# Clipping the ratio of layer 2 on ScalarE: a Relu with shifted logarithms in place of a VectorE maximum

## The chip, the cores and the metric

The kernel runs on one core of a Trainium2 chip. The core has five engines that work side by side, each through its own instruction queue and strictly in the order of that queue: TensorE (PE in the profile, its weight loads PEld), VectorE (DVE), ScalarE (ACT), GpSimd (POOL) and SyncE (SP, which issues most DMAs). They wait for each other through semaphores. The metric is the device time of one execution in microseconds (us), taken as the median of several runs; lower is better.

## What is computed

Four graph layers run one after another on 32 graphs of 512 nodes with 64 features; each layer is followed by x = layernorm(x + layer(x)). Layer 0 is a normalised neighbour mean, layer 1 a Chebyshev filter of order 4, layer 2 hyperbolic attention and layer 3 a weighted quantile of the neighbours with a small network behind it. The change lies in layer 2, which needs for every pair of nodes (i, j) the distance of the two points in the Poincaré ball:

```python
def _artanh(x):
    return jnp.arctanh(jnp.clip(x, -1.0 + 1e-07, 1.0 - 1e-07))

def logmap(p1, p2, c):
    sub = mobius_add(-p1, p2, c)
    sub_norm = _norm(sub)
    sqrt_c = c ** 0.5
    return 2.0 / sqrt_c / lambda_x(p1, c) * _artanh(sqrt_c * sub_norm) * sub / sub_norm
```

artanh(r) is half of ln(1 + r) - ln(1 - r). The clip keeps r below 1, so that the second logarithm stays finite. All 512 x 512 pairs of a graph need it, but the matrix is symmetric: the kernel computes the upper triangle in blocks (512 + 384 + 256 + 128 = 1280 columns on 128 partitions) and gets the rest by transposing.

## The kernel before

For each of the 32 graphs the kernel records the operations of seven lanes, in Python functions: `front` (loads, layers 0 and 1), `pairs` (layer 2's pair matrix), `tail` (the rest of layer 2), `graph`, `gather` and `sort` (layer 3's ranks, one-hot gather and sorting network), and for each pair of graphs `head` (the sorting network's narrow part, the network and the output). Helpers record them: `tt` (line 448, a VectorE operation on two tensors), `ts` (452, on one tensor and constants), `stt` (455), `act` (483, ScalarE), `mm` (502, matmul), `tr` (507, transpose), `gp` (POOL). Nearly every instruction of the profile therefore has a helper's line, and the tile's name tells what it is.

The order is not that of the recording. The class `Order` plans it at build time. It gives every operation a duration by formula (`ts` on f32: 0.07 + 0.52e-3 us per element; `act`: 0.12 + 0.83e-3 us per element, plus 0.09 for each bias or scale that is a tile), a due time from `STAGES` and a period of 80 us per graph, and then lets each engine take, whenever it is free, the ready operation with the earliest due time. The engines' queues are then pinned to that order. One more rule bears on PE: where the plan has a gap on PE, it puts filler matmuls on a scratch bank, `stay_active` (lines 1458 and 1459), one for each 0.11 us of the gap beyond its first 0.3 us. So the number of fillers in PE's queue tells how much waiting of PE the order was laid out with.

Around the change, in `pairs`: E holds the clipped-below squared distance, X its product with a denominator. The work is done in two parts of 640 columns (`parts2`). ScalarE makes R = X^-1/2 through Ln and Exp and W = R²/2; VectorE refines that with one Newton step (W·X, then R, each 128 x 640) and multiplies E by R, which gives minus the ratio r; then comes the clip; ScalarE takes both logarithms, into W and X; VectorE subtracts them and multiplies with R into Q. Q goes through PE (transposes of blocks, of `pairs_L`) to the attention weights. The tiles `EX`, `RW` and `Q` have one buffer each, so the next graph's pairs wait until this graph's have been read.

Of the kernel before, what the change touches and what calls it, by code (L numbers as in the profile page):

```python
# [8 lines left out]
F32 = mybir.dt.float32  # L9
# [5 lines left out]
AF = mybir.ActivationFunctionType  # L15
OP = mybir.AluOpType
# [4 lines left out]
P = 128  # L21
# [382 lines left out]
def tile_adj_resnorm(ctx: ExitStack, tc: tile.TileContext, x, adj, nodemask, w1k, b1k, att_w, att_b,  # L404
                     w1, b1, w2, b2, out):
    nc = tc.nc
# [12 lines left out]
    const = ctx.enter_context(tc.tile_pool(name="const", bufs=1))  # L419
# [7 lines left out]
    def width(a):  # L427
        n = 1
        for d in a.ap[1:]:
            n *= d[1]  # L430
        return n

    def vec(f, out, ins, one=False, scalars=(), reads=None, **kw):

        n = width(reads if reads is not None else out)
        tiles = [out] + list(ins)
        rate = 1.04e-3
        if not any(a.space == PSUM for a in tiles):
            half = all(a.dtype in (F16, BF16) for a in tiles)
            if one:  # L440
                rate = 0.26e-3 if half else 0.52e-3
            elif half:
                rate = 0.52e-3
        sc = [a for a in scalars if isinstance(a, bass.AP)]
        seq.op("DVE", 0.07 + n * rate + 0.065 * len(sc), 0.085, f, [out], list(ins) + sc)

    def tt(out, a, b, op):
        vec(lambda: nc.vector.tensor_tensor(out, a, b, op=op), out, [a, b])  # L448

    def ts(out, a, s1, s2, op0, op1=None):  # L450
        kw = {} if op1 is None else {"op1": op1}
        vec(lambda: nc.vector.tensor_scalar(out, a, s1, s2, op0=op0, **kw), out, [a], True, (s1, s2))  # L452

    def stt(out, a, s, b, op0, op1):
        vec(lambda: nc.vector.scalar_tensor_tensor(out, a, s, b, op0=op0, op1=op1), out, [a, b], False, (s,))  # L455
# [21 lines left out]
    def act(out, a, f, bias=None, scale=1.0, accum_out=None, after=None):  # L477
        sc = [x for x in (bias, scale) if isinstance(x, bass.AP)]
        kw = {k: v for k, v in (("bias", bias), ("accum_out", accum_out)) if v is not None}
        n = width(out)  # L480
        table = "exp" if f in (AF.Ln, AF.Exp) else "sig" if f in (AF.Sigmoid, AF.Tanh) else None
        seq.op("ACT", 0.12 + n * 0.83e-3 + 0.09 * len(sc) + (0.2 if accum_out is not None else 0.0),
             0.3, lambda: nc.scalar.activation(out, a, f, scale=scale, **kw), [out, accum_out], [a, after] + sc, table)  # L483
# [119 lines left out]
    ts(last, kf[:, 16:].unsqueeze(2).to_broadcast([P, K - 16, 8]), 2.0, 1.0, op0=OP.mult, op1=OP.add)  # L603
    mhalf = const.tile([P, T], F32, name="mhalf")
    nc.gpsimd.memset(mhalf, -0.5)
    tiny = const.tile([P, 1], F32, name="tiny")
    nc.vector.memset(tiny, 1e-36)
    onesb = const.tile([P, P], BF16, name="onesb")
    nc.vector.memset(onesb, 1.0)
    zero = const.tile([P, 2 * P], BF16, name="zero")  # L610
# [96 lines left out]
    def wide(name, tag=None):  # L707
        return seq.tile(pools["small"], [P, T, D], F32, name, 1, tag)
# [260 lines left out]
    def pairs(b, res):  # L969
# [65 lines left out]
        E, X = EX[:, 0, :], EX[:, 1, :]  # L1035
        RW = seq.tile(mid, [P, 2, NS], F32, "RW", 1)
        R, W = RW[:, 0, :], RW[:, 1, :]
        for j in range(T):
            n = N - j * P
            o = slice(OB[j], OB[j + 1])  # L1040
# [12 lines left out]
        for o in parts2:  # L1053

            tt(W[:, o], W[:, o], X[:, o], op=OP.mult)
            stt(R[:, o], W[:, o], -1.5, R[:, o], op0=OP.add, op1=OP.mult)
            tt(E[:, o], E[:, o], R[:, o], op=OP.mult)
            ts(E[:, o], E[:, o], -1.0 + 1e-7, None, op0=OP.max)
            act(W[:, o], E[:, o], AF.Ln, bias=1.0)
            act(X[:, o], E[:, o], AF.Ln, bias=1.0, scale=-1.0)  # L1060
        Q = seq.tile(mid, [P, T, N], F32, "Q", 1)
        for o in parts2:
            tt(W[:, o], W[:, o], X[:, o], op=OP.subtract)
        for j in range(T):
            o = slice(OB[j], OB[j + 1])
# [37 lines left out]
        v = wide("v")  # L1103
# [320 lines left out]
    with ExitStack() as fast:  # L1424
# [42 lines left out]
        for b in range(B):  # L1467
            if b % 2 == 0:
                both = {"ends": []}
            res = dict(both)  # L1470
            seq.batch = b
            for lane, f in (("front", front), ("pairs", pairs), ("graph", stage_graph), ("gather", gather), ("sort", sort)):
                seq.lane = lane
                f(b, res)
            both["ends"].append((res["slots"][1], res["x3"][0]))
            both.update(ohm=res["ohm"], ap=res["ap"])
            if b == B - 1:
                both["spots"] = spots(both["ends"])
            if b % 2:
                seq.lane = "head"  # L1480
                head(b, both)
# [144 lines left out]
    with tc.If(flagv > 0):  # L1626
        with ExitStack() as slow:
# [24 lines left out]
            for h in range(4):  # L1652
                t = cst.tile([P, T, QC * ROWS], BF16, name=f"parts{h}")
# [32 lines left out]
def build(inputs):  # L1686
    import numpy as np
    import concourse.bacc as bacc

    nc = bacc.Bacc("TRN2", target_bir_lowering=False, num_devices=1)  # L1690
    arrays, args = {}, []
    for name in _INS:
        a = np.ascontiguousarray(inputs[name])
        if a.dtype == np.bool_:
            a = a.view(np.uint8)
        arrays[f"in_{name}_dram"] = a
        args.append(nc.dram_tensor(f"in_{name}_dram", a.shape, mybir.dt.from_np(a.dtype), kind="ExternalInput").ap())
    args.append(nc.dram_tensor("out_0_dram", inputs["x"].shape, F32, kind="ExternalOutput").ap())
    with tile.TileContext(nc) as tc:
        tile_adj_resnorm(tc, *args)  # L1700
    return nc, arrays
# [8 lines left out]
```

## Time and profile before

| what | us |
| --- | --- |
| median of 3 runs (2572.68 to 2582.51) | 2580.22 |
| the profiled execution's own time | 2575.55 |
| its span, first to last instruction | 2573.7 |
| PE busy, share of the span | 2413.6 (94%) |
| DVE busy | 2382.1 (93%) |
| ACT busy | 1837.6 (71%) |
| POOL busy | 848.9 (33%) |
| granted TensorE clock, mean | 0.979 |

PE's busy time includes the fillers, and the ends of matmuls are modelled. A DVE or ACT record reaches some way into the next one of its engine: a record is longer than what the instruction costs in its queue. DMA plays no part: the queues' packets take 6.5% of the 16 DMA engines.

### The profile page before, as it was taken

The numbers are of one execution on the slowest core, as the hardware profiler recorded it, in microseconds if no ns is written. First come the engines' busy times: TensorE is split into PE (matmuls) and PEld (weight loads), VectorE is DVE, ScalarE is ACT, GpSimd is POOL, SyncE is SP. The second block draws the span as 40 slices with busy tenths as digits, with TensorE's granted clock in tenths as the row PEclk, the third lists the DMA queues.
The fourth block names the chain that finished last, engine by engine and source line by source line (L and its number), as shares of the span: only waits on it lengthen the run. The fifth ranks groups of instructions, "written<-read, shape, count | busy, mean of one in ns | idle before, by whom it ended". The sixth has DMA issues, their size and how long they took to land.

```text
span 2573.7 us, 56084 instructions
## 1 busy us (share of the span) xinstructions
PE 2413.6 (94%) x19895; PEld 1635.0 (64%) x19918; DVE 2382.1 (93%) x8937; ACT 1837.6 (71%) x4156; POOL 848.9 (33%) x2007
## 2 busy tenths in 40 slices
PE   7999989999999999999999999999999999999997
PEld 6766666656666666666666666666666666666555
DVE  4669999999999999999999999999999999999996
ACT  5766677777677777777677776877777777777761
POOL 1234434333234333323343433333333333333210
PEclk9999999999899999999999999998999999999998
DMA  1100000000000000000000000000000000000000
GB/s 39 36 22 21 22 14 13 24 22 26 20 15 19 16 26 22 24 10 22 22 20 26 22 22 22 12 22 20 26 22 18 16 18 24 20 12 3 8 5 8
DMA packets 119723, 49.98 MB, mean 19 GB/s; under 512 B 53740, under 2 KB 119436, under 8 KB 119436
## 3 DMA queue, kind: packets, MB, share of 16 engines
q1 hardware_dynamic: 118272, 46.15, 6.5%
q8 instruction: 158, 2.59, 0.4%
q14 instruction: 129, 1.06, 0.1%
q10 hardware_dynamic: 1164, 0.18, 0.0%
HBM read 37.93 MB, written 8.39 MB: 18 GB/s over the span
## 4 chain that ended last, share of the span: by engine, by line
DVE 73%; PE 20%; ACT 4%; issue 2%; POOL 1%; DMA 0%; ACTq 0%; DVEq 0%
DVE SB L448 17%; DVE SH L448 10%; DVE gather_oh L452 7%; PE pairs_bank L502 4%; DVE pairs_Q L448 4%; PE front_bank L502 4%; PE graph_bank L502 3%; PE gather_bank L502 3%; DVE pairs_RW L448 3%; DVE sort_prod L448 3%; DVE pairs_Wt L455 3%; DVE pairs_L L455 2%; PE head_bank L502 2%; DVE pairs_RW L455 2%; DVE pairs_EX L448 1%
## 5 line engine op out<-in xcount | busy, mean ns | idle before, releaser
L448 DVE TENSOR_TENSOR SB<-SB 128x92 f32<-128x92 f32 (+11 forms) x1424 | 566.8, 425 | 12.6
L502 PE MATMUL gather_bank<-gather_oh,tail_x3h 128*64 128x448 f16 (+5 forms) x5376 | 522.0, 319 | 5.6 <-ACT SB L483 4.2
L502 PEld LDWEIGHTS <-tail_x3h 128*64 128x64 bf16 x5376 | 294.7, 110 | 201.8 <-issue 95.7
L448 DVE TENSOR_TENSOR SH<-SH 128x128 f32<-128x128 f32 (+10 forms) x1744 | 341.6, 247 | 7.8
L502 PE MATMUL pairs_bank<-pairs_FT 67*128 67x512 f32 (+7 forms) x768 | 323.0, 522 | 16.6 <-DVE pairs_EX L455 9.4
L452 DVE TENSOR_SCALAR gather_oh<-graph_slot 128x256 f16<-128x256 f16 (+9 forms) x864 | 257.0, 337 | 19.1 <-PE gather_bank L502 17.0
L502 PE MATMUL front_bank<-front_AT,front_y 128*64 128x256 f32 x1536 | 193.5, 387 | 16.5 <-DVE front_y L448 15.5
L502 PEld LDWEIGHTS pairs_bank<-pairs_FT 67*128 67x128 f32 (+1 forms) x768 | 132.3, 196 | 85.3 <-issue 22.7
L502 PEld LDWEIGHTS front_bank<-front_AT,front_y 128*64 128x64 f32 x1536 | 118.1, 138 | 72.7 <-DVE front_y L448 18.9
L502 PE MATMUL graph_bank<-graph_perm,graph_V 128*128 128x512 f16 x512 | 141.6, 384 | 17.4 <-DVE graph_perm L452 16.0
L502 PEld LDWEIGHTS <-graph_nbT 128*128 128x128 f16 x1536 | 113.2, 99 | 57.7 <-issue 15.3
L1458 PE MATMUL PA<-zero 128*128 128x256 bf16 x1022 | 141.5, 280 | 0.1
L502 PEld LDWEIGHTS front_bank<-XA,front_AT 128*128 128x128 f32 x1024 | 126.2, 192 | 15.7 <-issue 6.6
L471 POOL TENSOR_TENSOR tail_nr<-tail_nr,tail_y 128x4 f32<-128x4 f32 x96 | 37.1, 386 | 285.6 <-DVE tail_y L461 230.4
L719 POOL TENSOR_TENSOR front_rs<-front_var,mhalf 128x4 f32<-128x4 f32 x64 | 81.5, 1273 | 145.7 <-DVE front_var L452 130.1
L502 PE MATMUL pairs_bank<-FLS,pairs_Wt 128*128 128x66 f32 x1024 | 123.8, 275 | 2.7 <-DVE pairs_Wt L455 2.2
L502 PEld LDWEIGHTS pairs_bank<-FLS,pairs_Wt 128*128 128x128 f32 x1024 | 119.4, 192 | 9.1 <-DVE pairs_Wt L455 7.1
L502 PE MATMUL front_bank<-XA,front_AT 128*128 128x65 f32 x1024 | 124.4, 272 | 0.3 <-ACT front_AT L483 0.3
L502 PEld LDWEIGHTS <-tabs 128*128 128x128 f16 x1296 | 78.6, 98 | 62.4 <-issue 49.6
L448 DVE TENSOR_TENSOR pairs_RW<-pairs_RW,pairs_EX 128x640 f32<-128x640 f32 x128 | 103.6, 816 | 13.7 <-ACT pairs_RW L483 9.2
L1458 PEld LDWEIGHTS <-zero 128*128 128x128 bf16 x1022 | 98.9, 101 | 23.8 <-issue 8.5
L483 ACT ACTIVATE SB<-gather_bank 128x448 f32<-128x448 f32 (+2 forms) x192 | 80.9, 439 | 45.0 <-PE gather_bank L502 44.2
(355 smaller groups left out, 6451.8 us busy)
## 6 DMA issues: line engine op xcount, KB each, us to landing
front_A<-in_adj_dram SPq DMA_DIRECT2D x128, 256.0 KB, 2.7
XA<-in_x_dram SPq DMA_DIRECT2D x32, 128.0 KB, 2.3
xs<-tail_x SPq DMA_DIRECT2D x32, 128.0 KB, 1.9
out_dram<-head_zo SPq DMA_DIRECT2D x31, 128.0 KB, 2.0
out_dram<-tail_ends SPq DMA_DIRECT2D x1, 128.0 KB, 2.1
wk<-in_L_gnn_weight_dram ACTq DMA_DIRECT2D x1, 64.0 KB, 3.1
w1s<-in_L_gnn_W_dram ACTq DMA_DIRECT2D x2, 32.0 KB, 1.9
attw<-in_L_gnn_att_W_dram ACTq DMA_DIRECT2D x2, 0.2 KB, 3.5
```

Source lines behind the costliest of these rows:

```text
L448: vec(lambda: nc.vector.tensor_tensor(out, a, b, op=op), out, [a, b])
L452: vec(lambda: nc.vector.tensor_scalar(out, a, s1, s2, op0=op0, **kw), out, [a], True, (s1, s2))
L455: vec(lambda: nc.vector.scalar_tensor_tensor(out, a, s, b, op0=op0, op1=op1), out, [a, b], False, (s,))
L471: gp(lambda: nc.gpsimd.tensor_tensor(out, a, b, op=op), out, [a, b])
L483: 0.3, lambda: nc.scalar.activation(out, a, f, scale=scale, **kw), [out, accum_out], [a, after] + sc, table)
L502: return nc.tensor.matmul(out, w, a, start=start, stop=stop)
L719: seq.op("POOL", 0.8, 0.6, lambda: nc.gpsimd.tensor_tensor(y, v, mhalf, op=OP.pow), [y], [v])
L1458: return nc.tensor.matmul(PA[:, 2 * P:], zero[:, :P], zero, start=False, stop=False)
```

## The change

The maximum on VectorE goes. In its place ScalarE takes Relu(E + 1 - 2^-23), which cuts at the same place up to a shift, and the shift is taken back in the biases of the two logarithms: ln(E' + 2^-23) and ln(-E' + 2 - 2^-23). These three biases are tiles of [128, 1], set once at the start; the logarithms' bias before was the constant 1.0.

```diff
-    tiny = const.tile([P, 1], F32, name="tiny")
-    nc.vector.memset(tiny, 1e-36)
+    def constant(name, v):
+        t = const.tile([P, 1], F32, name=name)
+        nc.vector.memset(t, v)
+        return t
+
+    tiny = constant("tiny", 1e-36)
+    least, under, double = constant("least", 2.0**-23), constant("under", 1.0 - 2.0**-23), constant("double", 2.0 - 2.0**-23)
@@ pairs, for o in parts2 @@
             tt(E[:, o], E[:, o], R[:, o], op=OP.mult)
-            ts(E[:, o], E[:, o], -1.0 + 1e-7, None, op0=OP.max)
-            act(W[:, o], E[:, o], AF.Ln, bias=1.0)
-            act(X[:, o], E[:, o], AF.Ln, bias=1.0, scale=-1.0)
+            act(E[:, o], E[:, o], AF.Relu, bias=under)
+            act(W[:, o], E[:, o], AF.Ln, bias=least)
+            act(X[:, o], E[:, o], AF.Ln, bias=double, scale=-1.0)
```

Since the planner sees other durations and another engine, it lays out a new order for all engines; no constant of the planner is changed.

## The prediction

> **What bounds the kernel now.** I read the page first: busy times, then the chain of waits.
>
> ```profile
> PE 2413.6 (94%) x19895; PEld 1635.0 (64%) x19918; DVE 2382.1 (93%) x8937; ACT 1837.6 (71%) x4156; POOL 848.9 (33%) x2007
> DVE 73%; PE 20%; ACT 4%; issue 2%; POOL 1%; DMA 0%; ACTq 0%; DVEq 0%
> ```
>
> VectorE and TensorE are both nearly full, and the chain runs 73% through VectorE and 20% through TensorE. A share over the whole span mixes start, steady run and end, so the second view is busy time by stretches (span, then PE, PEld, DVE, ACT, POOL, granted clock, DMA).
>
> ```profile
> 78.00:193.00 115.00, 110.29 (x895) 80.70 (x895) 76.83 (x253) 81.28 (x189) 33.55 (x95) 1.00 0.08 23
> 193.00:2445.00 2252.00, 2129.99 (x17529) 1428.89 (x17547) 2169.64 (x8065) 1664.04 (x3787) 784.83 (x1783) 0.98 0.07 19
> ```
>
> In the steady run DVE is busy for 2169.6 of 2252 us: 82 us idle, 3.7%. PE is idle for 122 us there, and its busy time holds fillers. So VectorE is the bound, but TensorE follows within a few per cent; there is no large reserve behind it. The third view is groups, for what the change touches and for the fillers.
>
> ```profile
> L452 DVE TENSOR_SCALAR pairs_EX<-pairs_EX 128x640 f32<-128x640 f32 x64 | 30.8, 483 | 0.2
> L483 ACT ACTIVATE pairs_RW<-pairs_EX,tiny 128x640 f32<-128x640 f32 x64 | 52.9, 828 | 15.7 <-DVE pairs_EX L455 15.1
> L483 ACT ACTIVATE pairs_RW<-pairs_EX 128x640 f32<-128x640 f32 x64 | 47.0, 734 | 37.7 <-DVE pairs_EX L452 37.3
> L1458 PE MATMUL PA<-zero 128*128 128x256 bf16 x1022 | 141.5, 280 | 0.1
> ```
>
> The first is the clip that goes; the second a Ln with a tile as its bias (828 ns), the third one without (734 ns); the fourth most of the fillers, 141.5 / 1022 = 0.138 us each. The timeline tells what a record costs in its queue:
>
> ```profile
> 1185.06 0.48 DVE L452 TENSOR_SCALAR pairs_EX<-pairs_EX 128x640 f32<-128x640 f32 x1
> 1185.47 0.15 DVE L455 SCALAR_TENSOR_TENSOR front_off<-front_mv,front_rs 128x4 f32<-128x4 f32 x1
> ...
> 1187.00 0.81 ACT L483 ACTIVATE pairs_RW<-pairs_EX,tiny 128x640 f32<-128x640 f32 x1
> 1187.72 0.72 ACT L483 ACTIVATE pairs_RW<-pairs_EX 128x640 f32<-128x640 f32 x1
> 1188.34 0.72 ACT L483 ACTIVATE pairs_RW<-pairs_RW 128x640 f32<-128x640 f32 x1
> ```
>
> The next VectorE instruction starts 0.41 us after the clip, not 0.48. On ScalarE 640 columns cost 0.72 us with a tile bias and 0.62 without.
>
> **The change part by part.** (1) VectorE loses 64 clips: 64 x 0.41 = 26.2 us (30.8 by whole records, the most it can be). They stand in the full queue, with 0.2 us of idle ahead of all of them: if the queue closes up, all of it is gained. Three more memsets of [128, 1] at the start cost some 0.1 us each by the row of a like memset (112 ns), under the weights' DMA that VectorE waits 2.5 us for.
>
> (2) ScalarE gains 64 Relus with a tile bias, 64 x 0.72 = 46.1 us, and 128 logarithms grow by 0.10: 12.8 us. The compiled order shows 58 table loads instead of 57 at each of two places: 2 x 1.28 = 2.6 us. Together 61.5 us, against 736 us in which ScalarE is idle: 71% becomes 74%. This load is hidden under the other engines. The Trainium skill (ScalarE: Activation LUTs, Rules for kernel authors) speaks against it: relu and maximum belong on VectorE, which is faster per element. The rows agree, 0.41 against 0.72 us; by the rule alone the change would lose 64 x 0.31 = 20 us, by the busy times alone it would win 26.
>
> (3) The chain within a graph grows. From E·R to both logarithms there were 0.41 + 0.62 us plus the last logarithm; now there are 0.72 + 0.72, plus a last one that is 0.10 longer: 0.51 us a part, 64 parts, 33 us if every microsecond were waited for, 0 if covered. The cover is the VectorE work that stands in the queue between E·R and W - X. Adding up the compiled order with the trace's durations, it was 5.1 us on average after the clip before, and is 5.9 us now; the need is now 0.72 + 0.72 + 0.83 = 2.3 us and some handover, and 5 of the 64 parts have under 3.0. VectorE waited there 4.1 us in four waits before. I take +2 for it, of 0 to 33. Whoever stands behind these logarithms on ScalarE (evacuations of `SB`, `graph_v`, `front_AT`) is 1 us later per part, which counts where PE waits for a bank: `gather_bank` for `SB` cost PE 4.2 us in all. +0 to +4, I take +1.
>
> (4) The order. POOL (2080 instructions) and SP (268) have the same instructions in both; DVE and ACT differ by what is named above; no DMA is added, and the loads of the next graph sit on SP as before. But the queues are laid out anew, and PE's shows one thing that is no accident of naming: 1236 + 175 fillers in place of 1022 + 118, so 271 more, in 210 runs instead of 170. Its other 17,232 matmuls are the same. Between the 1,980th and the 9,240th of PE's other instructions (a stretch of the first third) fillers go from 133 to 301; ahead of transposes of `pairs_L` from 37 to 89. An order that saved VectorE's 26 us would leave PE 26 us less to wait; this one is laid out with more waiting. The price from the trace: 271 x 0.138 = 37.4 us of filler matmuls, and 40 more runs leave at least the 0.3 us each that the rule does not fill, 12 us. That is +49 us if all of it is added to PE's time and nothing else of its 160 us of idle time shrinks. It is 0 if the fillers only collect short gaps that the order had anyway; then the gain of (1) stands.
>
> I weigh it so. For: PE's time is work plus waits and ends with the span, so more waiting with the same work is a later end. Against: fillers and VectorE's idle don't go together in the trace of before. In the row 2445:2509 fillers take 14.8 us of PE, and VectorE is idle for 1.3.
>
> ```profile
> 2381.00:2445.00 64.00, 60.76 (x485) 38.05 (x482) 62.48 (x208) 49.87 (x110) 18.54 (x34) 0.97 0.03 8
> 2445.00:2509.00 64.00, 60.65 (x521) 36.87 (x520) 62.66 (x272) 39.04 (x79) 12.34 (x28) 0.95 0.02 6
> ```
>
> The net effect, (1) included, lies between -26 + 3 = -23 us (only the queue closing up) and +49 us (all the waiting real). I take +22, a little nearer to the second: the count is a fact of the new program, while the queue's closing up is a hope. It asks that VectorE's idle in the steady run goes from 82 to 82 + 26 + 22 = 130 us, 5.7% of it. Some slices of before are that idle now (386 to 450: 5.3 of 64 us; 1094 to 1158: 5.4).
>
> The sum is against the profiled execution: 2575.6 + 22 = 2597.6 (span 2595.7). That execution was 4.7 us under the median of 2580.2; on the median's scale it is 2602.
>
> **The rivals.** *VectorE closes up.* For it: 73% of the chain, 3.7% idle, 0.2 us ahead of the clip, a cover of 5.9 us. Against: 271 fillers. It gives -23 us with all of the saving, -19 by the chain's share (0.73 x 26.2): some 2557 to 2561. This is the rival on the other side; it decides if VectorE's idle in the steady run stays under 82 + 13 us.
>
> *They cancel.* Half of the waiting is real, -23 + 25 = about 0, within 0.5% (13 us), which is about what a measurement of this kernel can tell from no change. For it: two engines near full, each with another's slack.
>
> *The longer chain is the bound.* If `pairs` set the pace (single buffers of EX, RW and Q), the full 33 us of (3) would count, and no saving: 2613. Against it: the logarithms' waits of 4.1 us, and the cover; ahead of ScalarE's first Ln it was the clip that came late (37.3 us), and that was VectorE's queue, which is now shorter.
>
> *The change doesn't do what it says.* Excluded as far as the program goes: the compiled VectorE queue has no clip left.
>
> **How the numbers follow.** Slower by over 0.5%: 0.60 (the forecast 0.52, the chain as bound 0.08). Within 0.5%: 0.25. Closing up: 0.15. The range reaches from 2564, which leaves out most of the closing-up case, to 2629, the +49 us on the median's scale: some 0.8 of the chance. Slower cases alone would lie in 2594 to 2629.
>
> **What would show it.** In the profile after: no `ts` on `pairs_EX`; 64 Relus with a bias at some 0.82 us, logarithms at 0.83; DVE busy near 2382 - 26 to 31 = 2351 to 2356, ACT near 1899; fillers 1236 and 175. The forecast is right if DVE's idle grows by about 48 us or more in all, most of it between 190 and 1000 us, behind PE or `pairs`. It is wrong if DVE's idle stays near 190 us in all: then the fillers only took the place of short gaps, and the span falls by the clip's own time.

## The result and the profile after

The changed kernel takes 2605.47 us (median of 7 runs, 2596.55 to 2610.25) against 2581.86 us before on the same chip: ratio 1.0095, 95% interval 1.0075 to 1.0115, so 24 us slower. The profiled execution took 2605.47 us with a span of 2603.4 us. The page first: busy times and the chain of waits.

```profile
PE 2436.9 (94%) x20167; PEld 1663.6 (64%) x20189; DVE 2360.0 (91%) x8876; ACT 1893.2 (73%) x4222; POOL 853.6 (33%) x2007
DVE 70%; PE 20%; ACT 6%; issue 2%; POOL 1%; DMA 0%; ACTq 0%; DVEq 0%
```

VectorE does 22.1 us less work (2382.1 to 2360.0), ScalarE 55.6 us more, and the span is 29.7 us longer: VectorE's idle time went from 191.6 to 243.4 us, by 51.8. (The two profiled executions lie 29.9 us apart, 6 more than the medians.) By stretches (the columns are the stretch and its length, then busy PE, PEld, DVE, ACT and POOL, the granted clock and DMA), before:

```profile
193.00:1029.00 836.00, 788.29 (x6484) 530.23 (x6488) 804.48 (x2971) 609.38 (x1384) 296.68 (x680) 0.98 0.07 20
1029.00:2445.00 1416.00, 1341.70 (x11047) 898.66 (x11059) 1365.16 (x5095) 1054.66 (x2404) 488.14 (x1103) 0.98 0.07 18
```

and after:

```profile
193.00:1029.00 836.00, 785.27 (x6582) 537.76 (x6587) 783.06 (x2911) 618.31 (x1389) 300.94 (x668) 0.98 0.07 20
1029.00:2445.00 1416.00, 1341.67 (x11000) 901.00 (x11013) 1342.85 (x5029) 1079.95 (x2414) 485.69 (x1113) 0.98 0.07 18
```

VectorE's idle grows by 21.4 us in the first stretch (31.5 to 52.9) and by 22.3 in the second (50.8 to 73.2), 3 us ahead of 193 and 5 behind 2445. The granted clock is the same, 0.98. What VectorE waits for, in us, times and the longest, in the table of waits after:

```profile
DVE gather_oh L452 <- PE gather_bank L502: 48.5, 32, 4.3
DVE pairs_RW L448 <- ACT pairs_RW L483: 14.5, 16, 2.2
DVE pairs_EX L455 <- PE pairs_bank L502: 11.4, 10, 2.6
DVE pairs_RW L448 <- ACT pairs_EX L483: 5.1, 5, 3.0
```

and before:

```profile
DVE gather_oh L452 <- PE gather_bank L502: 17.0, 14, 2.3
DVE pairs_RW L448 <- ACT pairs_RW L483: 9.2, 8, 1.8
DVE pairs_EX L455 <- PE pairs_bank L502: 8.3, 9, 1.8
DVE pairs_RW L448 <- ACT pairs_EX L483: 4.1, 4, 1.9
```

The greatest new wait has nothing to do with the clip. It is layer 3's one-hot tile `oh`, with two buffers: VectorE can write the next one only when PE has multiplied the one before last. It grows by 31.5 us. The waits of `pairs_RW` are two. For the second logarithm (`<- ACT pairs_EX`) it goes from 4.1 to 5.1 us. The other one (`<- ACT pairs_RW`, 9.2 to 14.5) is earlier in the chain: the product W·X waits for ScalarE's W = R²/2. In the experiments, where the logarithms have lines of their own, that wait stays with the helper's line. The groups show the added and the dearer operations at the sizes forecast:

```profile
L483 ACT ACTIVATE pairs_EX<-pairs_EX,under 128x640 f32<-128x640 f32 x64 | 52.7, 827 | 41.0 <-DVE pairs_EX L448 40.7
L483 ACT ACTIVATE pairs_RW<-pairs_EX,least 128x640 f32<-128x640 f32 x64 | 52.6, 825 | 0.6
L483 ACT ACTIVATE pairs_EX<-pairs_EX,double 128x640 f32<-128x640 f32 x64 | 52.6, 824 | 0.0
```

The fillers came as forecast too, 1236 and 175, and TensorE was busy with them for 195.4 us. These are the rows after, and the row of before that the forecast did not show:

```profile
L1463 PE MATMUL PA<-zero 128*128 128x256 bf16 x1236 | 171.8, 280 | 0.4 <-issue 0.2
L1464 PE MATMUL PA<-UC,identb 128*128 128x256 f16 x175 | 23.6, 273 | 0.9 <-ACT sort_ap L483 0.9
```

```profile
L1459 PE MATMUL PA<-UC,identb 128*128 128x256 f16 x118 | 16.9, 280 | 0.5 <-ACT sort_ap L483 0.5
```

### The profile page after: what moved, and what is told of

It is laid out like the page before. It is cut to its first block, busy times and chain, and to the rows that moved or that the text cites. A ratio compares the mean times of both kernels' runs of the same rounds, so it can differ in the third digit from the quotient of the medians.

```text
span 2603.4 us, 56633 instructions
## 1 busy us (share of the span) xinstructions
PE 2436.9 (94%) x20167; PEld 1663.6 (64%) x20189; DVE 2360.0 (91%) x8876; ACT 1893.2 (73%) x4222; POOL 853.6 (33%) x2007
## 4 chain that ended last, share of the span: by engine, by line
DVE 70%; PE 20%; ACT 6%; issue 2%; POOL 1%; DMA 0%; ACTq 0%; DVEq 0%
DVE SB L448 19%; DVE SH L448 10%; DVE gather_oh L452 6%; PE front_bank L502 4%; PE gather_bank L502 4%; DVE pairs_Q L448 4%; PE pairs_bank L502 4%; PE graph_bank L502 3%; DVE pairs_Wt L455 3%; DVE pairs_RW L448 3%; DVE sort_prod L448 2%; DVE pairs_L L455 2%; PE head_bank L502 1%; ACT pairs_RW L483 1%; DVE PRS L448 1%
## 5 line engine op out<-in xcount | busy, mean ns | idle before, releaser
L502 PE MATMUL gather_bank<-gather_oh,tail_x3h 128*64 128x448 f16 (+5 forms) x5376 | 511.4, 320 | 3.6 <-ACT SB L483 2.6
L448 DVE TENSOR_TENSOR SH<-SH 128x128 f32<-128x128 f32 (+11 forms) x1744 | 343.6, 246 | 9.3 <-ACT SH L483 1.5
L502 PE MATMUL pairs_bank<-pairs_FT 67*128 67x512 f32 (+7 forms) x768 | 316.4, 516 | 19.3 <-DVE pairs_EX L455 10.1
L452 DVE TENSOR_SCALAR gather_oh<-graph_slot 128x256 f16<-128x256 f16 (+9 forms) x864 | 253.7, 338 | 50.9 <-PE gather_bank L502 48.5
L1463 PE MATMUL PA<-zero 128*128 128x256 bf16 x1236 | 171.8, 280 | 0.4 <-issue 0.2
L1463 PEld LDWEIGHTS <-zero 128*128 128x128 bf16 x1236 | 120.1, 101 | 34.8 <-issue 16.7
L448 DVE TENSOR_TENSOR pairs_RW<-pairs_RW,pairs_EX 128x640 f32<-128x640 f32 x128 | 104.3, 816 | 20.0 <-ACT pairs_RW L483 14.5
L483 ACT ACTIVATE graph_V<-graph_bank 128x512 f16<-128x512 f32 x128 | 75.7, 592 | 56.6 <-PE graph_bank L502 56.0
```

The lines of the kernel that those rows point to most:

```text
L502: return nc.tensor.matmul(out, w, a, start=start, stop=stop)
L1463: return nc.tensor.matmul(PA[:, 2 * P:], zero[:, :P], zero, start=False, stop=False)
```

## The experiments

Theory A is that of the prediction: the operations themselves win, and the order that the planner lays out for them loses more. Theory B: the longer chain Relu, Ln, Ln on ScalarE loses, whatever the order. Theory C: the 271 added fillers themselves are the cost, through the TensorE time that they take.

### The operations and the order taken apart

`Order` gets a table `queue` that lets an operation be planned for one engine and emitted on another. Everything else of the order stays: the other instructions of the five queues keep the sequence of the kernel whose order is used.

The changed operations in the order of before:

```diff
-            e, fn = ops[i][0], ops[i][3]
+            e, fn = self.queue.get(i, ops[i][0]), ops[i][3]
...
-            ts(E[:, o], E[:, o], -1.0 + 1e-7, None, op0=OP.max)
+            seq.queue[len(seq.ops)] = "ACT"
+            vec(lambda e=E[:, o]: nc.scalar.activation(e, e, AF.Relu, bias=under), E[:, o], [E[:, o]], True)
```

(and the two logarithms with the biases `least` and `double`, planned at their old cost)

> The order is planned exactly as before (the clip as a VectorE operation with its old cost, the logarithms with their old cost), but the clip is emitted as the Relu on ScalarE and the logarithms with tile biases, each at the place that the plan gives it. Fillers stay 1140 in 170 runs. Theory A (the new order loses, the operations themselves win): VectorE's 26 us come free and little is lost, 2560 us, 0.6% to 1.0% faster than before. Theory B (the longer chain Relu, Ln, Ln loses, whatever the order): no faster than before, 2581 to 2613 us.

Measured: 2579.87 us, ratio 0.999 (0.9975 to 1.0006). No gain and no loss.

The old operations in the order of the changed kernel:

```diff
-            act(E[:, o], E[:, o], AF.Relu, bias=under)
+            seq.queue[len(seq.ops)] = "DVE"
+            seq.op("ACT", 0.12 + width(E[:, o]) * 0.83e-3 + 0.09, 0.3,
+                   lambda e=E[:, o]: nc.vector.tensor_scalar(e, e, -1.0 + 1e-7, None, op0=OP.max), [E[:, o]], [E[:, o]])
```

(and the two logarithms with the constant bias, planned as with tiles)

> The reverse: the order is planned exactly as in the changed kernel (1411 fillers in 210 runs), but the clip is emitted as the old VectorE maximum and the logarithms with the constant bias. Theory A: all of the loss is the order's, and VectorE's 26 us come on top of it, 2615 to 2632 us, 1.3% to 2% slower than before. Theory B: with the old operations the loss is gone, 2581 us, within 0.5% of before.

Measured: 2615.74 us, ratio 1.0138 (1.0115 to 1.0162). With not one of the changed operations in it, the new order is 1.4% slower than the old one. Theory B falls as the cause of the loss. The wait for `oh` follows the order, too; here it is in this kernel, and in the one before it (changed operations, old order):

```profile
DVE gather_oh L453 <- PE gather_bank L507: 47.3, 29, 4.3
DVE pairs_RW L449 <- ACT pairs_RW L484: 10.0, 12, 2.0
DVE pairs_RW L449 <- ACT pairs_EX L1072: 2.8, 2, 2.2
```

```profile
DVE gather_oh L453 <- PE gather_bank L507: 18.2, 16, 2.4
DVE pairs_RW L449 <- ACT pairs_EX L1071: 20.3, 21, 3.4
DVE pairs_RW L449 <- ACT pairs_RW L484: 13.9, 9, 2.9
```

But A was wrong in its other half: the operations by themselves gain nothing in the old order. The second fence shows where it goes. VectorE waits 20.3 us for the second logarithm (line 1071) to come back, against 4.1 before, and 13.9 against 9.2 for W = R²/2 ahead of it. Together that is 34.2 against 13.3: 20.9 us given back of the 22.8 us that VectorE worked less (2382.1 to 2359.3), 16.2 of them at the logarithm. The busy times of this run:

```profile
PE 2408.4 (93%) x19918; PEld 1638.2 (64%) x19918; DVE 2359.3 (92%) x8876; ACT 1891.8 (73%) x4220; POOL 839.5 (33%) x2007
```

### Are the fillers the cost?

```diff
-        seq.issue(80.0, STAGES, stay_active, 0.3)
+        seq.issue(80.0, STAGES, stay_active, 0.6)
```

> The changed kernel with the same order of all other instructions, but a filler only for gaps beyond 0.6 us instead of 0.3: 909 fillers in place of 1411. Theory A (the fillers only mark the waiting): the time stays at 2605 us within 0.3%. Theory C (the filler matmuls themselves cost time, 0.138 us each on TensorE): 502 fewer give up to 69 us back, 2536 to 2580 us. If the granted clock falls, both are disturbed.

Measured: 2604.95 us, ratio to before 1.008 (1.0057 to 1.0104), with the granted clock at 0.971 in its profile. And the kernel before with 0.1 in that place:

> The kernel before with the same order of all other instructions, but a filler for gaps beyond 0.1 us instead of 0.3: 1534 fillers in place of 1140. Theory A: within 0.3% of before, 2575 to 2590 us. Theory C: 394 more fillers cost up to 54 us, 2600 to 2635 us.

Measured: 2580.81 us, ratio 0.9995 (0.9984 to 1.0006). The busy times of the two, fewer fillers and then more:

```profile
PE 2407.4 (92%) x19687; PEld 1626.4 (62%) x19687; DVE 2360.2 (90%) x8876; ACT 1892.4 (73%) x4222; POOL 845.8 (32%) x2007
```

```profile
PE 2453.0 (95%) x20312; PEld 1674.2 (65%) x20312; DVE 2382.4 (92%) x8937; ACT 1837.7 (71%) x4156; POOL 847.2 (33%) x2007
```

TensorE's busy time moves by 29.5 us down and 39.4 up (from 2436.9 and 2413.6), the kernels' times by nothing beyond the intervals. As the cause of the loss Theory C falls: the order is slow with 502 fillers fewer, and the old one is not slower with 394 more. In the run with fewer, VectorE's wait for `oh` is 55.4 us, not less than the 48.5 of the changed kernel.

That a filler costs TensorE nothing is not shown, since the granted clock moved with their number: 0.970 to 0.977 in the runs with fewer against 0.977 to 0.985 in those of the changed kernel, and 0.979 to 0.987 with more against 0.975 to 0.980 for before on the same chip. Executions of one and the same kernel tell what that may hide: before took 2572.88 us at a clock of 0.981 and 2593.08 at 0.971, some 2 us for 0.001. By the middle clocks of these runs (0.973 against 0.979, 0.9845 against 0.976) that is an estimated 12 to 17 us, or 0.02 to 0.04 us for a filler, which the clock gives back; the full 0.138 it is not.

### What is VectorE's time worth, and what eats it?

The clip left out, in the order of before:

```diff
-            ts(E[:, o], E[:, o], -1.0 + 1e-7, None, op0=OP.max)
+            vec(lambda: None, E[:, o], [E[:, o]], True)
```

(and `Order` passes over an operation that emits nothing)

> The clip is left out altogether (part of the computation is missing); the order is planned as before with the clip in it, and nothing is emitted in its place; the logarithms are those of before. This measures what VectorE's 26 us are worth without any load on ScalarE. If the queue closes up: 2558 us, 1.0% faster than before. If other waits of the same order take the place: within 0.5% of before, 2572 to 2584 us; then the Relu's longer chain is not what ate the gain.

Measured: 2558.36 us, ratio 0.9917 (0.9886 to 0.9949). 0.83% of 2578.4 us is 21.4 us, for 64 x 0.41 = 26.2 us taken out of VectorE's queue: with nothing put in its place, four fifths of it are gained. So the queue does close up, and it was the change's ScalarE half that ate the gain in the old order. Its chain or its load? Here the same 64 Relus run after the second logarithm, where nothing waits for their result (the clip is left out and the logarithms have the constant bias, as in the run just above):

```diff
+            planned(X[:, o], E[:, o], 0, lambda x=X[:, o], e=E[:, o]: [nc.scalar.activation(x, e, AF.Ln, bias=1.0, scale=-1.0),
+                                                                     nc.scalar.activation(e, e, AF.Relu, bias=under)])
```

> The order as before and the clip left out as in the run without a clip (part of the computation is missing), but ScalarE runs the same 64 Relus with a tile bias on E right after the second logarithm, where nothing waits for their result: ScalarE's load of 46 us is there, its 0.72 us per part in the chain is not. If the chain's length ate VectorE's gain: near the run without a clip, 2556 to 2564 us, 0.6% to 0.9% faster than before. If the load in ScalarE's queue did: near the old order with the Relu in the chain, 2575 to 2582 us, no faster than before.

Measured: 2561.3 us, ratio 0.9932 (0.9907 to 0.9957). ScalarE's load is there (the Relus' group, and the engines' busy times):

```profile
L1073 ACT ACTIVATE pairs_EX<-pairs_EX,under 128x640 f32<-128x640 f32 x64 | 53.1, 829 | 2.1
```

```profile
PE 2392.6 (94%) x19918; PEld 1626.3 (64%) x19918; DVE 2359.5 (93%) x8876; ACT 1885.4 (74%) x4220; POOL 850.0 (33%) x2007
```

Against the kernel without it (0.9917) it costs nothing that the intervals can tell: the difference is 0.15%, uncertain by some 0.4%, so a few us for the load are not excluded. Against the Relu in the chain (0.999) it is faster by 0.6%, clear of both intervals. VectorE's wait for the second logarithm goes along: 20.3 us with the Relu in the chain, 7.6 with it beside and 4.6 without (beside, then without):

```profile
DVE pairs_RW L451 <- ACT pairs_EX L1072: 7.6, 9, 3.0
```

```profile
DVE pairs_RW L451 <- ACT pairs_EX L486: 4.6, 4, 2.4
```

What ate the gain is, for the most part, the length of the chain: 0.72 us of Relu, and 0.10 for each logarithm's tile bias (which this run leaves out; the two were not tried apart with the Relu in place), in an order whose VectorE queue was spaced for two plain logarithms.

### How much does an order decide?

One constant of the planner moved, with the operations of before, and then twice with the changed operations:

```diff
-    HOP = 0.1
+    HOP = 0.09
```

> The kernel before, same operations, with one constant of the planner moved (a handover of 0.09 us instead of 0.10): another order with 1538 fillers in place of 1140. Theory A with the price seen so far (an order with 271 more fillers cost 34 us with the old operations, 0.125 us per filler): 398 more cost up to 50 us, 2605 to 2634 us. Theory B (orders are alike, the operations decide): 2581 us within 0.5%.

Measured: 2617.11 us, ratio 1.0164 (1.0127 to 1.0201).

```diff
-    STAGES = {"front": (-0.6, -0.5), "pairs": (1.2, 1.3), "tail": (0.2, 1.5), ...
+    STAGES = {"front": (-0.6, -0.5), "pairs": (1.1, 1.2), "tail": (0.2, 1.5), ...
```

> The changed kernel with one constant of the planner moved (the pairs lane due between 1.1 and 1.2 periods instead of 1.2 and 1.3): 1242 fillers, 102 more than before. Theory A: 13 us for the order less 0 to 10 us for the operations, 2583 to 2597 us, faster than the changed kernel as it is. Theory B: 2605 us like the changed kernel.

Measured: 2584.18 us, ratio 1.0025 (1.0008 to 1.0042): the same instructions as the changed kernel but for 169 fillers, 0.7% faster through another order.

```diff
-        seq.issue(80.0, STAGES, stay_active, 0.3)
+        seq.issue(80.5, STAGES, stay_active, 0.3)
```

> The changed kernel with the period at 80.5 us instead of 80: 1793 fillers, 653 more than before. Theory A: 82 us for the order less 0 to 10 us for the operations, 2640 to 2665 us. Theory B: 2605 us.

Measured: 2630.33 us, ratio 1.02 (1.0169 to 1.023).

| operations | order | fillers | DVE waits for PE's `gather_bank`, us | ratio to before |
| --- | --- | --- | --- | --- |
| of before | before | 1140 | 17.0 | 1 |
| of before | changed | 1411 | 47.3 | 1.0138 |
| of before | HOP 0.09 | 1538 | 51.3 | 1.0164 |
| changed | before | 1140 | 18.2 | 0.999 |
| changed | pairs 1.1 | 1242 | 40.7 | 1.0025 |
| changed | changed | 1411 | 48.5 | 1.0095 |
| changed | period 80.5 | 1793 | 59.9 | 1.0200 |

Within each set of operations the time rises with the fillers, but not at one price: the last row's order was put at 82 us, and the kernel came out some 52 us slower than before. Over the old order with the same operations, a filler more stands for 0.13 us (36 / 271) and 0.11 (42 / 398) with those of before, and for 0.10 (27 / 271) and 0.08 (54 / 653) with the changed ones. The wait for `oh` tells slow orders from fast ones, but not by how much: the row with pairs at 1.1 has 22.5 us more of it than the changed operations in the old order, and takes 0.35%, some 9 us, longer.

Eighteen orders laid out for the operations of before with one constant moved have between 1150 and 1538 fillers; all of them are above the 1140 of the order that it has. (They were planned and not run, but for the one with 1538.) So that one looks like a picked order, and an edit that the planner sees is likely to give it up.

### Versions without the second half

These leave out the half of the change that puts a Relu on ScalarE. First the clip left out, with a bias of 1 + 2^-20 from a tile on the first logarithm, in the order of before:

```diff
-            act(W[:, o], E[:, o], AF.Ln, bias=1.0)
+            planned(W[:, o], E[:, o], 0, lambda w=W[:, o], e=E[:, o]: nc.scalar.activation(w, e, AF.Ln, bias=above))
```

(`ts` is gone as in the kernel without a clip)

> A candidate for use: no clip on either engine, the order as before, and the first logarithm takes the bias 1 + 2^-20 from a tile, which keeps its argument positive where the ratio rounds to just over 1 (the clip to 1 - 1e-7 itself is left out). ScalarE gains 64 x 0.10 = 6 us. Theory A: as without a clip, plus at most 3 us, 2556 to 2562 us, faster than both kernels by 0.7% to 1%. Theory B: 2575 to 2585 us.

Measured: 2552.65 us, ratio 0.9901 (0.9874 to 0.9928), below the range expected. One logarithm's tile bias alone, in a chain without the Relu, costs nothing that shows against 0.9917. The bias moves only one of the two logarithms, so that for small ratios, those of the diagonal above all, their difference is no longer the ratio's: it is a measurement of time and not a version for use. The same operations, planned for themselves, with `HOP` at 0.09:

> The same operations as the candidate, but planned for themselves, with a handover of 0.09 us instead of 0.10: 1148 fillers in 172 runs, the fewest of 16 settings that were laid out. Theory A (fillers gauge the order): 8 fillers more than before cost 1 us, 2555 to 2566 us, like the candidate in the old order.

Measured: 2567.91 us, ratio 0.995 (0.9929 to 0.9971), slower than in the old order by 0.5% at 8 fillers more, and above the range expected. As a gauge the count tells 1%, not half of that.

Last, the clip behind the logarithm, inside a subtraction that is there anyway:

```diff
-            tt(W[:, o], W[:, o], X[:, o], op=OP.subtract)
+            stt(W[:, o], W[:, o], -15.942385, X[:, o], op0=OP.max, op1=OP.subtract)
```

(ahead of it `ts` is gone as in the kernel without a clip; the order is that of before)

> The clip is moved behind the first logarithm and into the subtraction that is there anyway: max(W, ln 2^-23) - X as one VectorE instruction on two tensors and a constant, in place of W - X. No instruction is added on any engine, the clip is gone from VectorE's queue, and the chain has no Relu; the order is as before. The row of a like instruction (816 ns, as the plain subtraction) says that it costs the same. Theory A: like the run without a clip, 2553 to 2562 us, 0.7% to 1.1% faster than before, and faster than both kernels. Theory B: 2575 to 2585 us.

Measured: 2558.83 us, ratio 0.9924 (0.9909 to 0.994). It beats both kernels, by 0.8% and by 1.7%. The subtraction (second row) costs what the plain product of the same shape does (first row; ns are least, median, most):

```profile
L451 DVE TENSOR_TENSOR pairs_RW<-pairs_RW,pairs_EX x64: 807/816/827, 88.9 to 2382.2; 128x640 f32<-128x640 f32 x64
L458 DVE SCALAR_TENSOR_TENSOR pairs_RW<-pairs_RW,pairs_EX x64: 786/815/826, 95.6 to 2388.7; 128x640 f32<-128x640 f32 x64
```

What the first logarithm, and the maximum after it, give for a ratio that rounds to 1 or above is shown by no run here.

## Why the prediction was right

The forecast was 2602 us; 2605.5 were measured, in the range and with the sign that had 0.60. Its steps:

(1) VectorE's 26.2 us. The clips are gone, and busy time fell by 22.1. Taken alone the gain is 21.4 us, near the "closing up" case. With the change's ScalarE half it was less: in the new order 1.0138 - 1.0095 = 0.43% (uncertain by 0.3%), 11 us, and in the old order 3 us, which the interval does not tell from nothing. The working had -23 net of the small terms. This term was sized too large.

(2) ScalarE's added load of 61.5 us, costed at nothing because ScalarE is idle for 736: 55.6 were measured, and the run with the Relus beside the chain shows no cost that can be told from none. Right, as far as that goes. The Trainium skill (ScalarE: Activation LUTs, Rules for kernel authors) gives relu and max to VectorE, as the faster engine per element; its figure is for bf16. For these 640 columns of f32 VectorE is the faster one here too (0.41 against 0.72 us in the queue). But the kernel's time doesn't follow: with the order kept, the Relu on ScalarE is no slower than the maximum on VectorE (0.999), and in the new order it is 0.43% faster.

(3) The chain: +2 us of 0 to 33, by a cover of 5.9 us. In the new order VectorE waits 5.1 us for the second logarithm, against 2.8 with the old operations in that order: 2.3 us, as forecast. (For W = R²/2 it is 14.5 against 10.0; the forecast had no term for that.) But the price belongs to the order: in the old order it is 20.3 against 4.1, 16.2 us of the 33 that were its upper end, and with the wait for W enough to cancel the saving. The traces of these orders show why. The VectorE work between E·R and W - X comes to some 4 us on average in the old order, with 16 or 17 of the 64 parts under 3.0 us; in the new order it is some 5 us, with 5 to 7 parts under 3.0.

(4) The order. It was bounded by 0 and +49 us from 271 fillers at 0.138 and 40 runs at 0.3, and the forecast's +22 asks some 45 of it; the order alone cost 0.0138 x 2584 = 36 us with the old operations, and 1.0095 - 0.999 = 1.05%, 27 us, with the changed ones. So -11 + 36, or -3 + 27, is the measured sum of some +24. The forecast had both terms' signs and both sizes too large, and the two errors cancel: that 22 lies so near is in part luck, the more so as it was picked between bounds 72 us apart. Of the +49, the fillers' busy time is there (195.4 against 158.4 us, 37.0), but TensorE's whole busy time grew by only 23.3 us and its idle time by 6.4, not 12; how much of that is the modelling of matmul ends isn't known. What the forecast did not name is the place: it looked at the transposes of `pairs_L`, and the wait that grew most is that of `oh` for PE's gather, 31.5 of 51.8 us. It also put most of the loss between 190 and 1000 us; 21.4 of the 51.8 lie there, the rest is spread over the run.

The idle time that the forecast asked of VectorE in the steady run, 130 us of 2252, came out at 126.1 in the same stretch. The prediction took the fillers as a mark of waiting; the two runs on their number show that the time does not follow it, with the clock moving along.

Why the gather comes later against VectorE in these orders is open: a third buffer of `oh` would change the order as well and was not tried.

## What to carry to other kernels

In a kernel whose whole order is planned at build time, an edit has two prices, that of its operations and that of the new order, and they can be taken apart by planning one kernel and emitting the other. (They don't simply add up: the order cost 36 us with the old operations and 27 with the changed ones.) Whoever tries an operation in such a kernel should first try it in the old order; a picked order can hide a gain of 1%. And work that is moved off a full engine onto an idle one is free only where it does not lengthen a chain that comes back to the full engine: here 64 Relus in the chain, with the logarithms' dearer biases, cost 0.6% more than the same Relus beside it (0.999 against 0.9932), and beside it they cost nothing that could be told from leaving them out (0.9917).

## What the runs showed of the hardware

The time that a ScalarE instruction adds by reading its bias from a [128, 1] tile was 94 ns on 640 columns (828 against 734 ns), and 0.10 us in the queue's pace (0.72 against 0.62). The Trainium skill (ScalarE: Activation LUTs, What ACT_TABLE_LOAD costs) gives about 93 ns for each such operand, which agrees. Unexpected was how little 400 matmuls more in TensorE's queue matter: 1534 fillers instead of 1140 raise TensorE's busy time to 2453.0 us, 95% of the span, and the kernel's time stays within 0.2%, at a granted clock that rose from 0.976 to 0.9845 (medians of the runs).
